# Eight images through four layers on one core: background work drawn evenly, and in chunk-sized tiles

## The chip, the cores and the metric

The kernel runs on one core of a Trainium2 chip. The metric is device time in microseconds (us), the median of three runs. The engines are PE (TensorE, matrix products, with weight loads shown as PEld), DVE (VectorE), ACT (ScalarE), POOL (GpSimd) and SP (SyncE); POOL and SP here mostly issue DMA transfers. All data are fp32.

## What is computed

The input is x of shape (8, 384, 32, 32): 8 images, 384 channels, 32 x 32 pixels. Four layers follow each other. Cut to what matters:

```python
# layer 0: Mamba in two directions, plus a gated 3x3 depthwise convolution
xn = rmsnorm(x, norm_w)
u, z = split(in_proj(xn))
u = silu(causal_conv1d(u, 4 taps))
dt, Bm, Cm = split(x_proj(u))
delta = softplus(dt_proj(dt) + dt_b)
# twice: over the pixels in order and in reverse
h[t] = exp(delta * A) * h[t-1] + (delta * u) * Bm     # 16 states a channel, scanned over 1024 pixels
y = (sum over states of h * Cm + u * D) * silu(z)
x1 = x + res_scale * (sigmoid(dwconv3x3(xn)) * xn + scale_mod * out_proj(y_forward + y_backward))
# layer 1, for each image: conv block, linear attention, MLP
x1 = conv1x1(bn(dwconv3x3(conv1x1(bn(x1))))) + x1
x2 = x1 + proj(linear_attention(qkv(x1)))
x2 = x2 + mlp(layernorm(x2))                          # 384 -> 1536 -> 384, GELU
# layer 2: seven depthwise kernels (13x13 and dilated ones), each with its batch norm, summed
# layer 3: 1x1 convolution + skip, 13x13 depthwise convolution + scaled skip, GELU
```

Layers 0 and 1 work image by image. Layers 2 and 3 work on all images at once, after the last image, as matrix products with Toeplitz matrices that are built from the convolution kernels.

## The kernel before

The scan of layer 0 is the backbone: 48 units an image (2 directions, 2 halves of 512 pixels, 3 chunks of 128 channels, 4 groups of states). A unit is, on DVE, a product, a scan and a second product, each over 2048 columns, with four ACT exponentials ahead and four small PE reductions behind:

```python
                da = das[i % len(das)]
                for j in range(4):
                    nc.scalar.activation(
                        da[:, SEG * j + 1 : SEG * (j + 1)], dlt[:, j, :], AF.Exp,
                        scale=neg_a[:, 4 * c + j, r : r + 1],
                    )
                du = sp.tile([P, 4 * SEG + 1], FP, tag="du", name=f"du_{b}_{i}", bufs=4)
                # ... first / last / carry cut
                nc.vector.tensor_mul(
                    flat(1)[:, :, 0:HALF], vt, bct[r][:, 0:1, :].to_broadcast([P, 4, HALF])
                )
                if pend is not None:
                    product(pend)
                if d == 0:
                    s = slice(0, 4 * SEG)
                    nc.vector.tensor_tensor_scan(du[:, s], da[:, s], du[:, s], 0.0, ALU.mult, ALU.add)
                else:
                    s = slice(1, 4 * SEG + 1)
                    nc.vector.tensor_tensor_scan(
                        du[:, s][:, ::-1], da[:, s][:, ::-1], du[:, s][:, ::-1], 0.0, ALU.mult, ALU.add
                    )
            # product(), called one unit later:
                nc.vector.tensor_mul(dv, dv, cct[:, 1:2, :].to_broadcast([P, 4, HALF]))
                for j in range(4):
                    nc.tensor.matmul(
                        acc[32 * j : 32 * j + 32, :], selt, dv[:, j, :],
                        start=False, stop=(r == NR - 1), skip_group_check=True,
                    )
```

Everything else of layers 0 and 1 is background: generators that issue a piece and yield its cost. `front(b)` is the input side of an image (norm, in_proj, convolutions, deltas), `layer1(b)` the second layer, `fold()` puts norms into weights and, at its end, makes the Toeplitz sources for layers 2 and 3 with `kernels()`. The loop over images draws them beside the scan:

```python
        for _ in front(0):
            tick()
        tick(everything=True)
        rounds = 4 * NC * NR
        for b in range(B):
            work = []
            if b + 1 < B:
                work.append((front(b + 1), 94))
            if b == 0:
                work.append((fold(), 30))
            if b > 0:
                work.append((layer1(b - 1), 290))
            need = sum(n for _, n in work)
            steps = (cost for g, _ in work for cost in g)
            done = 0
            for i, _ in enumerate(scan(b)):
                tick()
                while done < need * (i + 1) / rounds:
                    cost = next(steps, None)
                    if cost is None:
                        break
                    done += cost
            for _ in steps:
                tick()
            tick(everything=True)
        for _ in layer1(B - 1):
            tick()
        tick(everything=True)
```

The last part of `kernels()` copies windows of the merged kernels, DRAM to DRAM, 64 transfers of 24 x 32 x 224 elements, with a yield of cost 0:

```python
        NP = 24
        for g_d, t_d in ((g2_d, tp2_d), (g3_d, tp3_d)):
            for at in range(0, C // 2, NP):
                for q in range(2):
                    for e in range(2):
                        one_k = g_d[2 * at + e, q]
                        win = bass.AP(
                            one_k.tensor, one_k.offset,
                            [[4 * TG * (KP // 2), NP], [KP // 2, H], [1, TP]],
                        )
                        lo = 2 * H * q + H * e
                        nc.gpsimd.dma_start(t_d[at : at + NP, lo : lo + H, :], win)
                    yield 0
```

The background's tiles: half images with three chunks in one `a6` buffer, chunks in `t2`, weights in `w`.

```python
N_A6, N_T2, N_W, N_IM = 7, 10, 5, 6
# ...
        def t2(name):
            return sp.tile([P, HALF], FP, tag="t2", name=name, bufs=N_T2)

        def a6(name):
            return sp.tile([P, NC, HALF], FP, tag="a6", name=name, bufs=N_A6)

        def wtile(ap, name):
            t = sp.tile([P, NC, C], FP, tag="w", name=name, bufs=N_W)
            nc.gpsimd.dma_start(t, ap.rearrange("(k p) o -> p k o", p=P))
            return t
# ... in front(b):
            for e in range(2):
                w = wtile(inproj_t[:, e * C : (e + 1) * C], f"win_{b}_{e}")
                for h in range(2):
                    t = a6(f"uz_{b}_{e}_{h}")
                    for m in range(NC):
                        ps = psum(f"in_{b}_{e}_{m}_{h}")
                        dense(ps, w, m, xn[h])
                        if e == 0:
                            nc.scalar.copy(t[:, m, :], ps)
                        else:
                            nc.scalar.activation(t[:, m, :], ps, AF.Silu)
                        yield 3
                    if e == 0:
                        nc.gpsimd.dma_start(uo[:, :, 3 + h * HALF : 3 + (h + 1) * HALF], t)
                    else:
                        nc.gpsimd.dma_start(zv[b][:, :, bass.ts(h, HALF)], t)
# ... in layer1(b):
            for h in range(2):
                for m in range(NC):
                    ps = psum(f"c2_{b}_{m}_{h}")
                    dense(ps, w, m, dws[h])
                    t = t2(f"c2_{b}_{m}_{h}")
                    nc.scalar.activation(t, ps, AF.Identity, bias=biasc[:, m, :])

                    def residual(o=xx[h][:, m, :], t=t):
                        nc.vector.tensor_add(o, o, t)

                    defer(0, residual)
                    yield 3
# ... and at the end of each half's MLP:

                def last(h=h, acc=acc):
                    for m in range(NC):
                        o = xx[h][:, m, :]
                        nc.vector.scalar_tensor_tensor(
                            o, acc[m], vec("mlp_b2", m), o, ALU.add, ALU.add
                        )
                        # ... store to x2, cut
                defer(0, last)
```

Pieces that end on DVE are deferred (`defer(n, fn)`): they are issued n + 1 ticks later, and a tick comes with each scan unit. A scheduler then sets the final order on each engine, in which instructions wait for buffers and data in that engine's own queue.

## Time and profile before

| what | value |
|---|---|
| median of 3 runs | 6233.76 us (6221.53 to 6239.03) |
| span of the profiled execution | 6238.1 us |
| instructions in it | 52842 |
| DMA | 425913 packets, 1060.24 MB, mean 170 GB/s |
| mean granted TensorE clock | 0.864 of full speed |
| DVE scans (L771 and L774) | 2 x 192, 4.43 us each |
| DVE products (L764 and L686) | 2 x 384, 2.28 us each |
| first scan of images 0 to 7 at | 239, 721, 1475, 2087, 2699, 3310, 3922, 4531 us |

The page gives each engine's busy time as a share of the span, then 40 slices of it: a digit is the busy share of a slice in tenths. PEclk is the granted clock of TensorE, in tenths. An engine that is idle costs nothing unless the work that ends last waits for it. In views of stretches, a row is: from and to in us, its length, then busy time and number of instructions of PE, PEld, DVE, ACT and POOL, the granted clock, the busy share of the 16 DMA engines, and GB/s. In the view of waits, a row is: who waited, `<-` for whom, us in total, how many times, and the longest. The view of one line gives durations in ns (least, median, most), its waits, and, for a transfer, the time from issue to landing.

### The profile page before, as it was taken

Reading aid. Unit: us, or ns where it says so; the run is one execution under the profiler, and the core shown is the slowest. Engines: PE = TensorE matmul, PEld = TensorE weight load, DVE = VectorE, ACT = ScalarE, POOL = GpSimd, SP = SyncE. Lnnn points to the kernel's source line nnn. Section 1 sums busy time; section 2 is a strip of 40 time slices with the busy share of each in tenths; the row PEclk is TensorE's granted clock in tenths of the full one; section 3 lists DMA queues with packets and bytes.
Section 4 is the critical chain, followed back from the end, with each engine's and each line's share of the span. In section 5 each row is a group of like instructions: output and inputs, shape, how many; then the busy total and the mean of one; then the engine's idle time right before and its main releaser. Section 6 shows DMA issues by size and latency. Waiting matters only on the chain. (4 is left out here: it accounts for less than half of the span.)

```text
span 6238.1 us, 52842 instructions
## 1 busy us (share of the span) xinstructions
PE 4982.4 (80%) x19054; PEld 2193.0 (35%) x19054; DVE 4002.6 (64%) x2768; ACT 2789.8 (45%) x3891; POOL 1134.3 (18%) x1781
## 2 busy tenths in 40 slices
PE   4665407888789978898889789978989779898899
PEld 1111202333233323332333233323323224398498
DVE  0599943797779777977897789778978941000200
ACT  1655414455745574557355745574544523000211
POOL 4210223101210121013101310131010010111133
PEclk8776557899788978997899789979989889899999
DMA  9664696435643564466446643664363341399699
GB/s 294 203 193 135 213 306 195 146 122 152 228 144 122 158 224 142 139 161 228 126 146 174 217 134 124 186 219 127 122 181 109 131 118 41 79 221 216 208 215 198
DMA packets 425913, 1060.24 MB, mean 170 GB/s; under 512 B 58141, under 2 KB 108549, under 8 KB 425653
## 3 DMA queue, kind: packets, MB, share of 16 engines
q0 software_dynamic: 185792, 679.20, 37.6%
q1 hardware_dynamic: 210192, 354.31, 18.5%
q10 hardware_dynamic: 29668, 23.36, 1.6%
q8 instruction: 151, 2.47, 0.2%
q14 instruction: 110, 0.89, 0.0%
HBM read 807.16 MB, written 293.47 MB: 176 GB/s over the span
## 5 line engine op out<-in xcount | busy, mean ns | idle before, releaser
L751 ACT ACTIVATE da<-dlt,neg_a 128x512 f32<-128x512 f32 x1536 | 1000.2, 712 | 1063.4 <-DVE du L774 556.6
L764 DVE TENSOR_TENSOR du<-vr,bct 128x2048 f32<-128x2048 f32 x384 | 874.3, 2284 | 15.8 <-DMA vr<-v_d 9.8
L686 DVE TENSOR_TENSOR du<-du,bct 128x2048 f32<-128x2048 f32 x384 | 877.5, 2286 | 3.8
L771 DVE TENSOR_TENSOR_SCAN du<-da,du 128x2052 f32<-128x2052 f32 x192 | 849.1, 4427 | 40.5 <-ACT da L751 37.2
L774 DVE TENSOR_TENSOR_SCAN du<-da,du 128x2052 f32<-128x2052 f32 x192 | 848.2, 4426 | 6.2
L688 PE MATMUL acc<-du,selt 128*32 128x512 f32 x3072 | 606.8, 690 | 279.3 <-DVE du L686 279.3
L1000 PE MATMUL mo<-hm,w 128*128 128x512 f32 x1152 | 558.4, 626 | 61.8 <-ACT hm L998 59.1
L490 PE MATMUL mf<-ln,w 128*128 128x512 f32 x1152 | 551.3, 613 | 0.6 <-DVE ln L986 0.6
L499 PE MATMUL lc<-lc_i,t 96*32 96x512 f32 x1152 | 258.7, 860 | 170.4 <-DMA lc_i<-xn_d 167.6
L490 PE MATMUL in<-xn,win 128*128 128x512 f32 x576 | 264.4, 616 | 134.1 <-DMA win<-in_inproj_t 124.5
L499 PE MATMUL c<-ut,t 128*32 128x512 f32 x768 | 250.1, 804 | 141.1 <-ACT dl L650 54.8
L1000 PEld LDWEIGHTS mo<-hm,w 128*128 128x128 f32 x1152 | 219.2, 197 | 380.9 <-issue 246.3
L499 PE MATMUL dw<-dw_i,t3b 96*32 96x512 f32 x1152 | 265.9, 827 | 106.0 <-DMA dw_i<-h_d 95.4
L490 PEld LDWEIGHTS mf<-ln,w 128*128 128x128 f32 x1152 | 219.9, 196 | 321.5 <-issue 318.3
L312 PE MATMUL cv_b<-xt_b,toep 128*64 128x256 f32 x2688 | 302.4, 385 | 36.2 <-DMA xt_b<-xp_d 17.3
L688 PEld LDWEIGHTS acc<-du,selt 128*32 128x32 f32 x3072 | 100.1, 116 | 630.0 <-DVE du L686 359.4
L312 PE MATMUL cv_a<-xt_a,toep 128*64 128x256 f32 x2688 | 300.1, 383 | 24.6 <-issue 24.5
L312 PEld LDWEIGHTS cv_b<-xt_b,toep 128*64 128x64 f32 x2688 | 291.9, 194 | 47.2 <-issue 41.6
L998 ACT ACTIVATE hm<-mf,biasf 128x512 f32<-128x512 f32 x192 | 130.4, 687 | 397.9 <-PE mf L490 396.9
L312 PEld LDWEIGHTS cv_a<-xt_a,toep 128*64 128x64 f32 x2688 | 291.2, 194 | 33.1 <-issue 32.2
L751 ACT ACT_TABLE_LOAD x217 | 278.4, 1283 | 8.2 <-DVE du L771 4.5
L595 DVE TENSOR_TENSOR lg<-lg,xn 128x512 f32<-128x512 f32 x48 | 32.9, 686 | 338.9 <-ACT lg L592 338.9
(212 smaller groups left out, 6183.4 us busy)
## 6 DMA issues: line engine op xcount, KB each, us to landing
dlt<-dl_d SPq DMA_DIRECT2D x384, 256.0 KB, 5.8
vr<-v_d SPq DMA_DIRECT2D x384, 256.0 KB, 4.6
bct<-bc_d SPq DMA_DIRECT2D x256, 256.0 KB, 4.1
ut<-u_d POOLq DMA_DIRECT2D x192, 257.5 KB, 4.9
lc_i<-xn_d POOLq DMA_DIRECT2D x192, 228.8 KB, 5.8
dw_i<-h_d POOLq DMA_DIRECT2D x192, 228.8 KB, 4.3
tp_d<-g_d POOLq DMA_DIRECT2D x64, 672.0 KB, 20.1
w<-w_d POOLq DMA_DIRECT2D x64, 576.0 KB, 4.7
```

The costliest lines, as they stand in the source:

```text
L312: nc.tensor.matmul(ps[2 * H * e : 2 * H * (e + 1), 0:BW], tp[:, 2 * (g % (GB // 2)) + e, :, :, t].rearrange("p c j -> p (c j)"), rhs, star ...
L490: nc.tensor.matmul(ps, w[:, k, m * P : (m + 1) * P], rhs[k] if isinstance(rhs, list) else rhs[:, k, :], start=(k == 0), stop=(k == NC - 1),)
L499: nc.tensor.matmul(ps[32 * j : 32 * j + 32, :], lhs(j, i), rhs(j, i), start=(i == 0), stop=(i == taps - 1), skip_group_check=True,)
L595: nc.vector.tensor_mul(rows(lc), rows(lc), xn[h][c])
L686: nc.vector.tensor_mul(dv, dv, cct[:, 1:2, :].to_broadcast([P, 4, HALF]))
L688: nc.tensor.matmul(acc[32 * j : 32 * j + 32, :], selt, dv[:, j, :], start=False, stop=(r == NR - 1), skip_group_check=True,)
L751: nc.scalar.activation(da[:, SEG * j + 1 : SEG * (j + 1)], dlt[:, j, :], AF.Exp, scale=neg_a[:, 4 * c + j, r : r + 1],)
L764: nc.vector.tensor_mul(flat(1)[:, :, 0:HALF], vt, bct[r][:, 0:1, :].to_broadcast([P, 4, HALF]))
L771: nc.vector.tensor_tensor_scan(du[:, s], da[:, s], du[:, s], 0.0, ALU.mult, ALU.add)
L774: nc.vector.tensor_tensor_scan(du[:, s][:, ::-1], da[:, s][:, ::-1], du[:, s][:, ::-1], 0.0, ALU.mult, ALU.add)
L998: nc.scalar.activation(hm, ps, AF.Gelu, bias=biasf[:, NC * i + f, :])
L1000: nc.tensor.matmul(acc[m], wb[:, f, m * P : (m + 1) * P], hm, start=(i == 0 and f == 0), stop=(i == FF // C - 1 and f == NC - 1),)
```

## The change

The aim is to give each scan unit about the same background. The input side of the next image and the second layer of the previous one are now drawn side by side, whichever has used the smaller share of its cost, with costs set to 108 and 310 in place of 94 and 290, and drawn up by the last unit but one. The Toeplitz part leaves `fold()` for a generator of its own, `prepare()`, of cost 64, that runs beside image 1, with 2 a yield. So that both kinds of background can be alive at once, half-image tiles become chunks: `uz`, `xr` and `fr` take `t2` buffers, and each chunk has its own transfer. The scan's small tiles get a pool of their own (`s2`). To pay for this, there is one weight buffer less, one `bct` buffer less, and a narrower zero tile, so that pads are cleared in pieces of 384 columns. The residual of `c2` is issued a tick later, and forced before its first reader.

```diff
-N_A6, N_T2, N_W, N_IM = 7, 10, 5, 6
+N_A6, N_T2, N_S2, N_W, N_IM = 7, 11, 3, 4, 6
 ...
                         lo = 2 * H * q + H * e
                         nc.gpsimd.dma_start(t_d[at : at + NP, lo : lo + H, :], win)
-                    yield 0
+                    yield 2
 ...
-        zero = wp.tile([P, HALF], FP, tag="zero", name="zero")
+        zero = wp.tile([P, C + NC + 1], FP, tag="zero", name="zero")
         nc.gpsimd.memset(zero, 0.0)
         for i in range(2):
             for t, n in ((xn_d, IMG), (u_d, UL), (h_d, IMG)):
                 pads = t[i].rearrange("(c p) i -> p c i", p=P)
                 for c in range(NC):
-                    for a in range(0, n, HALF):
-                        e = min(n, a + HALF)
+                    for a in range(0, n, C):
+                        e = min(n, a + C)
 ...
+        def s2(name):
+            return sp.tile([P, HALF], FP, tag="s2", name=name, bufs=N_S2)
 ...
-                    t = a6(f"uz_{b}_{e}_{h}")
                     for m in range(NC):
                         ps = psum(f"in_{b}_{e}_{m}_{h}")
                         dense(ps, w, m, xn[h])
+                        t = t2(f"uz_{b}_{e}_{h}_{m}")
                         if e == 0:
-                            nc.scalar.copy(t[:, m, :], ps)
+                            nc.scalar.copy(t, ps)
+                            nc.gpsimd.dma_start(uo[:, m, 3 + h * HALF : 3 + (h + 1) * HALF], t)
                         else:
-                            nc.scalar.activation(t[:, m, :], ps, AF.Silu)
+                            nc.scalar.activation(t, ps, AF.Silu)
+                            nc.gpsimd.dma_start(zv[b][:, m, bass.ts(h, HALF)], t)
                         yield 3
-                    if e == 0:
-                        nc.gpsimd.dma_start(uo[:, :, 3 + h * HALF : 3 + (h + 1) * HALF], t)
-                    else:
-                        nc.gpsimd.dma_start(zv[b][:, :, bass.ts(h, HALF)], t)
 
 
             t3 = tapw(taps3, f"t3_{b}")
             for h in range(2):
-                xr = a6(f"xr_{b}_{h}")
-                nc.gpsimd.dma_start(xr, xv[b][:, :, bass.ts(h, HALF)])
                 for c in range(NC):
+                    xr = t2(f"xr_{b}_{h}_{c}")
+                    nc.gpsimd.dma_start(xr, xv[b][:, c, bass.ts(h, HALF)])
                     ps = conv3(xn_d, b % 2, h, c, t3, f"lc_{b}_{h}_{c}")
                     lc = t2(f"lg_{b}_{c}_{h}")
                     nc.scalar.activation(lc, ps, AF.Sigmoid, bias=vec("dw_b0", c))
 
                     def local(h=h, c=c, lc=lc, xr=xr):
                         nc.vector.tensor_mul(rows(lc), rows(lc), xn[h][c])
-                        nc.vector.scalar_tensor_tensor(
-                            xr[:, c, :], lc, rs, xr[:, c, :], ALU.mult, ALU.add
-                        )
-                        if c == NC - 1:
-                            nc.gpsimd.dma_start(x1v[b][:, :, bass.ts(h, HALF)], xr)
+                        nc.vector.scalar_tensor_tensor(xr, lc, rs, xr, ALU.mult, ALU.add)
+                        nc.gpsimd.dma_start(x1v[b][:, c, bass.ts(h, HALF)], xr)
 
 ...
-                fr = a6(f"fr_{b}_{h}")
-                nc.sync.dma_start(fr, x1v[b][:, :, cols])
                 w = wtile(outproj_t, f"wo_{b}_{h}")
                 for m in range(NC):
                     ps = psum(f"op_{b}_{m}_{h}")
                     dense(ps, w, m, g)
-                    nc.vector.scalar_tensor_tensor(
-                        fr[:, m, :], ps, rsm, fr[:, m, :], ALU.mult, ALU.add
-                    )
-                nc.gpsimd.dma_start(x1v[b][:, :, cols], fr)
+                    fr = t2(f"fr_{b}_{h}_{m}")
+                    nc.sync.dma_start(fr, x1v[b][:, m, cols])
+                    nc.vector.scalar_tensor_tensor(fr, ps, rsm, fr, ALU.mult, ALU.add)
+                    nc.gpsimd.dma_start(x1v[b][:, m, cols], fr)
 
 ...
-                        t = sp.tile([P, 2, HALF], FP, tag="bct", name=f"bct_{b}_{d}_{h}_{e}", bufs=5)
+                        t = sp.tile([P, 2, HALF], FP, tag="bct", name=f"bct_{b}_{d}_{h}_{e}", bufs=4)
 ...
+
+        def prepare():
             large = lambda name: sp.tile([P, NC * C], FP, tag="w", name=name, bufs=N_W)
             yield from kernels(t2, large)
 ...
-                    defer(0, residual)
+                    res[h].append(defer(1, residual))
 ...
+                for e in res[h]:
+                    force(e)
 ...
-                work.append((front(b + 1), 94))
+                work.append([front(b + 1), 108, 0])
+            if b > 0:
+                work.append([layer1(b - 1), 310, 0])
             if b == 0:
-                work.append((fold(), 30))
-            if b > 0:
-                work.append((layer1(b - 1), 290))
-            need = sum(n for _, n in work)
-            steps = (cost for g, _ in work for cost in g)
+                work.append([fold(), 30, 0])
+            if b == 1:
+                work.append([prepare(), 64, 0])
+            need = sum(n for _, n, _ in work)
             done = 0
             for i, _ in enumerate(scan(b)):
                 tick()
-                while done < need * (i + 1) / rounds:
-                    cost = next(steps, None)
+
+                while work and done < need * (i + 1) / (rounds - 1):
+                    w = min(work, key=lambda w: w[2] / w[1])
+                    cost = next(w[0], None)
                     if cost is None:
-                        break
+                        work.remove(w)
+                        continue
+                    w[2] += cost
                     done += cost
-            for _ in steps:
-                tick()
+            for w in work:
+                for _ in w[0]:
+                    tick()
```

More of the change, by code (lines that the diff above doesn't have):

```diff
@@ L478, in defer, with force @@
         def defer(n, fn):
-            late.append([n, fn])
+            e = [n, fn]
+            late.append(e)
+            return e
+        def force(e):
+            if e in late:
+                late.remove(e)
+                e[1]()
         def tick(everything=False):
@@ L695, in product @@
                 if d == 0:
-                    yt = t2(f"yt_{b}_{h}_{c}")
+                    yt = s2(f"yt_{b}_{h}_{c}")
                     nc.scalar.copy(yt, acc)
@@ L699, in product @@
                     return
-                zt = t2(f"zr_{b}_{h}_{c}")
+                zt = s2(f"zr_{b}_{h}_{c}")
                 nc.sync.dma_start(zt, zv[b][:, c, cols])
@@ L742, in scan @@
                     acc = accp.tile([P, HALF], FP, tag="acc", name=f"acc_{b}_{d}_{h}_{c}")
-                    yt = t2(f"y0_{b}_{d}_{h}_{c}")
+                    yt = s2(f"y0_{b}_{d}_{h}_{c}")
                     nc.sync.dma_start(yt, (udv if d == 0 else yfv)[b][:, c, cols])
@@ L858, in layer1 @@
             w = wtile(c2_d, f"c2_{b}")
+            res = [[], []]
             for h in range(2):
```

## The prediction

> **What bounds the kernel now.** I read the page first. Its line of busy times and its slices say that no engine is full:
>
> ```profile
> PE 4982.4 (80%) x19054; PEld 2193.0 (35%) x19054; DVE 4002.6 (64%) x2768; ACT 2789.8 (45%) x3891; POOL 1134.3 (18%) x1781
> ...
> PE   4665407888789978898889789978989779898899
> DVE  0599943797779777977897789778978941000200
> PEclk8776557899788978997899789979989889899999
> DMA  9664696435643564466446643664363341399699
> ```
>
> The fine structure repeats every four slices, and slice 6 (about 780 to 940 us) is a hole in PE and DVE while DMA is full. So the eight images are the unit to read in. I placed the cuts at the first forward scan (L771) of each image and asked for the busy time of each stretch:
>
> ```profile
> core 0: us, PE busy (x) PEld busy (x) DVE busy (x) ACT busy (x) POOL busy (x), PEclk, DMA share, GB/s
> 0.00:239.00 239.00, 109.84 (x326) 34.84 (x326) 30.62 (x83) 63.76 (x88) 92.56 (x161) 0.78 0.84 263
> 239.00:721.00 482.00, 276.48 (x928) 80.97 (x929) 470.31 (x312) 275.17 (x388) 76.14 (x134) 0.69 0.55 181
> 721.00:1475.00 754.00, 480.06 (x1570) 179.02 (x1569) 494.55 (x347) 312.49 (x441) 158.83 (x240) 0.77 0.62 193
> ...
> 2096.00:2708.00 612.00, 525.65 (x1658) 191.04 (x1658) 492.25 (x314) 343.71 (x467) 103.69 (x173) 0.88 0.53 164
> ...
> 4541.00:5055.00 514.00, 431.06 (x1363) 163.29 (x1362) 452.17 (x264) 245.04 (x340) 52.22 (x80) 0.91 0.44 132
> ```
>
> Image 0 has only the next image's input side beside its scan and is DVE-bound (470 of 482). Image 1 takes 754. Images 2 to 6 take 610 to 621 each, with PE at 526 and DVE at 492: 120 us of DVE idleness per image. Image 7 takes 514. Then 356 for the last second layer and 827 for the convolutions. Within one steady image, by quarters of its 48 scan units:
>
> ```profile
> 2096.00:2274.00 178.00, 152.43 (x502) 53.83 (x503) 127.20 (x87) 94.78 (x120) 40.62 (x67) 0.88 0.64 190
> 2274.00:2449.00 175.00, 138.87 (x439) 41.96 (x434) 126.37 (x83) 104.56 (x151) 41.66 (x78) 0.80 0.58 185
> 2449.00:2587.00 138.00, 125.72 (x429) 53.99 (x427) 125.19 (x89) 72.10 (x110) 7.19 (x11) 0.94 0.33 112
> 2587.00:2708.00 121.00, 108.62 (x299) 41.27 (x296) 113.49 (x58) 72.26 (x88) 14.22 (x19) 0.96 0.54 155
> ```
>
> The first half, where the leftover of the MLP and all of the input side run, is slow (178 and 175) at a lower granted clock; the second half is near DVE's own pace. What DVE waits for in that image:
>
> ```profile
> DVE xx L1009 <- PE mo L1000: 24.2, 1, 24.2
> DVE du L763 <- PE acc L688: 20.8, 5, 6.8
> DVE xx L867 <- ACT c L864: 16.8, 6, 5.3
> DVE dl L661 <- ACT sp L656: 16.8, 3, 13.1
> DVE lg L595 <- ACT lg L592: 11.9, 4, 7.4
> ```
>
> All but the second are a small background operation that stands in DVE's queue before its input is there, with the scan behind it. Last, the Toeplitz copies of image 1:
>
> ```profile
> L239 POOL DMA_DIRECT2D tp_d<-g_d x64: 828/835/886, 722.2 to 919.5; - x64
> ...
> DMA to landing us min/median/max: 5.2/20.1/28.8
> ```
>
> Between 755 and 945 us DMA is busy 0.96 of the time and DVE 89 of 190 us; the longest single waits there are 130 us (DVE for the sigmoid) and 126 us (PE for `win`).
>
> **What the Trainium skill says.** "Trace Analysis", section Optimization Strategy: where the most-contended engine changes over time, "performance may be improved by interleaving those regimes". The trace agrees that there are such regimes: the quarters above. "TensorE: Matmul & The Clock Gate", Part 1, has the clock depend on recent PE activity; the trace agrees in direction (0.80 in the quarter with PE at 79%, 0.96 in the one at 90%). "DMA: Bandwidth & Descriptors", Issuing engines are not separate DMA queues: all queues share 16 engines, so spreading the copies frees no bandwidth, it only moves it; here 64 copies of 672 KB, 43 MB. "ScalarE: Activation LUTs", What ACT_TABLE_LOAD costs: about 1283 ns a switch; the trace has 1283.
>
> **The change part by part.**
>
> *Even draw.* The built instruction orders (no times in them) show what the scheduler made of it. Before, the input side's PE work of image b+1 stands in units 3 to 15 and layer 1 from unit 15 into unit 3 of the next image. After, in images 3 to 6, the input side runs from unit 1 to unit 47, the MLP from 26 to 47, and its last matmuls end at unit 0 of the next image. The work is the same. PE work at full clock in a steady image, busy times clock by quarter: 152.4 x 0.88 + 138.9 x 0.80 + 125.7 x 0.94 + 108.6 x 0.96 = 468 us. Quarters 3 and 4 get through 118.2/138 = 104.3/121 = 0.86 of it per us with DVE at 91 to 94%. If the whole image ran like that: 468/0.86 = 544 us, in which DVE's 492 would be 90%. The evenness is not perfect: one lump of about 56 us of PE work stands between the reductions of units 8 and 9 in the order. DVE can run only some three units ahead (four `du` buffers), about 35 us, so it loses some 20 us there, of which I count 11. Steady image: 555 against 613, four of them (3 to 6): gain 4 x 58 = 232.
>
> *Image 7.* It has only layer 1 beside it. It loses the leftover MLP of the image before at its start (a wait of 24 us as above): 514 to 490, gain 24.
>
> *Toeplitz in image 1, and what it drags along.* Gained is the hole: 754 - 613 = 141 at most. But the new order is not even there. The copies stand in clumps of 6 to 8 at units 23, 27, 31, 35 and 47, and the last ten or so lie in image 2. Around them PE's order has lumps: I tallied the matmuls between successive reductions with the mean times of the steady image (0.92 us a built 512-column matmul, 0.44 an `lc` one, 0.7 a `kv` one) and got about 62, 64, 66 and 64 us in image 1 and 54, 94 and 90 us in image 2, to which some 90 us of PE work of image 1 is pushed. Each costs DVE its length less 35: 27 + 29 + 31 + 29 + 19 + 59 + 55 = 249. With DVE's own 2 x 492, and 65 for DMA crowding (the 43 MB at the 297 GB/s of the hole are 145 us of DMA on top of 0.53 x 613 = 325 in a 640 us image, 0.73 share; I take under half as felt): 984 + 249 + 65 = about 1300 for the two, against 754 + 621 = 1375. Gain 75.
>
> *Chunk tiles.* Same bytes, more transfers: 165 to 185 issues on the POOL queue per steady image, 20 x 0.6 us = 12 us of POOL, which is busy 104 of 612. Hidden. The half-image tiles no longer hold `a6` buffers while background of both kinds is alive, which is what makes the even draw possible. One fewer weight buffer (4) and one fewer `bct` buffer cost no wait that I can find in the order.
>
> *Table loads.* 81 to 91 per steady image in the order, 10 x 1.28 = 13 us of ACT at 56% busy: hidden.
>
> *Residual deferred by one tick.* Takes part of the 16.8 us of `xx L867`; already in the rate above.
>
> *Before image 0.* The smaller zero tile makes 12 more pad transfers, and chunks 14 more issues: 27 x 0.6 = 16 us of POOL in a 239 us stretch that waits mostly for landings; I add 6. Image 0 stays at DVE's pace, 482. The last layer and convolutions stay at 1183.
>
> Sum: 245 + 482 + 1300 + 4 x 555 + 490 + 1183 = 5920, on a span that was 6238; the median was 5 us lower than the span, which I leave.
>
> **The rivals.**
>
> *PE becomes the bound and nothing is won in the steady images.* PE is busy 526 of 612 now. At an unchanged clock it would need 526 us and some friction: 590 an image, total about 6060. For it: PE at 90% or more in the best windows already. Against: the low clock and waits of the second quarter, which mixing should lift.
>
> *The clumps turn into a new hole.* If POOL, which issues its queue in order and waited 110 us in total for earlier Toeplitz copies, holds up image loads behind each clump, images 1 and 2 together cost 1450 instead of 1300: total 6070.
>
> *Everything mixes well.* Steady images at 520 (DVE 95%), images 1 and 2 at 1180: 245 + 482 + 1180 + 2080 + 475 + 1183 = 5645. For it: image 0 shows DVE at 98% beside background. Against: image 0 has less than half the PE work.
>
> *More `t2` users starve the pool.* 11 buffers serve the chunks, the MLP's activations and the deltas at once; a wait for a buffer would show as ACT waiting for POOL or DMA. It would cost tens of us per image and bring the total to 6150.
>
> **Range and chances.** The steady images decide: four images at plus or minus 20 us are 80, images 1 and 2 plus or minus 100, the rest 20; together about 130 either way, slightly wider on the slow side since two rivals lie there: 5780 to 6080. Faster by over 2% means under 6109. Only the starved pool, or two of the slow rivals together, lead above it: 0.89 faster, 0.09 within 2%, 0.02 slower.
>
> **What would show it.** In the changed profile: no window near 780 to 940 us with DMA full and PE empty; starts of images 3 to 7 about 555 apart, with their quarters within 20 us of each other; the wait `DVE xx <- PE mo` of 24 us per image gone; mean granted clock above 0.90 in images 3 to 6; images 1 and 2 still the longest, about 650 each, with PE lumps in them. I am wrong if the steady images stay over 590, if image 1 is under 580, or if the last 1183 us change by more than 15.

## The result and the profile after

| | before | after |
|---|---|---|
| median of 4 runs each | 6236.40 us (6221.53 to 6279.01) | 6067.57 us (6063.13 to 6068.56) |
| ratio | | 0.9717, 95% interval 0.9669 to 0.9765 |
| mean granted clock | 0.864 | 0.877 |

The change gains 169 us where 316 were predicted. The time lies inside the range (5780 to 6080), near its slow end. From first scan to first scan of consecutive images, and then to the end, in us:

| | start | 0 | 1 | 2 | 3 | 4 | 5 | 6 | 7 | last layer and convolutions |
|---|---|---|---|---|---|---|---|---|---|---|
| before | 239 | 483 | 753 | 621 | 612 | 611 | 612 | 610 | 514 | 1183 |
| predicted | 245 | 482 | 1300 for 1 and 2 | | 555 | 555 | 555 | 555 | 490 | 1183 |
| after | 247 | 479 | 738 | 711 | 559 | 553 | 551 | 557 | 486 | 1187 |

Every entry is within 5 us of the prediction but one: images 1 and 2, 1449 us for 1300. (The list of first scans ahead of the prediction is 9 to 10 us early from image 3 on; they stand at 2096, 2708, 3319, 3931 and 4541 us, and the row "before" is worked out from these.) The slices of the page, of 152 us each, show both halves of this:

```profile
PE   3665546675479989898998999898978879798899
...
DVE  0499995565674897998899789978989921000200
...
PEclk8676767787789989898999899898989979899999
```

Counted from 1, slices 15 to 32 are images 3 to 7, with PE and DVE at seven tenths or more throughout. Slices 7 to 13 are where DVE's 9s are missing, in images 1 and 2. The hole of before (DMA full, PE and DVE empty) is not among them: from 780 to 940 us DVE is full now, and DMA at 0.60.

Stretches of the changed kernel from first scan to first scan, for images 1, 2 and 4 (columns as in the prediction):

```profile
726.00:1464.00 738.00, 451.38 (x1451) 162.48 (x1452) 486.90 (x342) 286.79 (x400) 145.49 (x224) 0.76 0.54 172
1464.00:2175.00 711.00, 567.67 (x1835) 209.61 (x1835) 502.11 (x329) 388.93 (x521) 137.79 (x232) 0.88 0.55 168
2733.00:3287.00 554.00, 494.24 (x1664) 179.90 (x1663) 492.65 (x316) 358.41 (x480) 113.54 (x194) 0.94 0.60 182
```

Image 4 (2733 to 3287) takes 554 us with DVE at its old 493 and PE at 494 instead of 526, at a clock of 0.94 instead of 0.88: 526 x 0.88 and 494 x 0.94 are both about 463 us at full clock, so it is the same work at a higher clock. The Trainium skill ("TensorE: Matmul & The Clock Gate", Part 1) has the clock follow the recent activity of PE. The trace agrees in direction: 0.94 with PE busy for 89% of the image, 0.88 with 86% before. Its largest DVE wait, in the view of waits (who, for whom, us in total, times, longest):

```profile
DVE du L764 <- PE acc L693: 21.4, 4, 15.4
```

The 24.2 us for `mo` of the MLP are gone (0.4 us are left). The wait of 21 us for the reduction is the lump between units 8 and 9, here 15.4 us once.

Images 1 and 2 are no less busy on DVE (487 and 502), but idle for 251 and 209 us. Cut into eighths, the pair reads as follows (the first, the second and the seventh):

```profile
726.00:910.00 184.00, 90.52 (x302) 24.07 (x302) 183.93 (x143) 66.38 (x102) 35.32 (x59) 0.67 0.59 191
910.00:1095.00 185.00, 115.35 (x420) 55.86 (x421) 81.39 (x47) 59.36 (x91) 27.34 (x40) 0.79 0.43 140
...
1820.00:1998.00 178.00, 174.67 (x684) 75.42 (x682) 88.67 (x77) 103.79 (x134) 38.96 (x69) 0.97 0.42 131
```

For the first 184 us DVE is full and PE gets work for half of the time, at a clock of 0.67: too little background stands in the order there. In the next eighth DVE is busy for 81 of 185 us. In the seventh PE is at 98% and DVE at 50%. What DVE waits for in image 1, and the largest single wait of image 2, as DVE's timeline has it (start, duration, operation, and in brackets the idle time before it with its releaser):

```profile
DVE du L766 <- PE acc L693: 91.5, 4, 33.6
DVE kv L912 <- PE kvs L906: 35.8, 1, 35.8
DVE du L764 <- PE acc L693: 30.9, 2, 17.4
```
```profile
1871.89 0.06 DVE L766 MEMSET du<- 128x4 f32 x1 [52.64 <-PE acc L693]
```

In PE's timeline from 1819 to 1872 us there are `kv`, `kvs` and `in` matmuls back to back, and the next reduction (`acc`) comes after them. It is the first of the two large lumps that the built order holds in image 2 (94 and 90 us in the prediction), and the wait is 52.6 us where the prediction had 94 - 35 = 59. POOL, on the other hand, hardly waits for its copies:

```profile
L239 POOL DMA_DIRECT2D tp_d<-g_d x64: 831/862/1017, 759.9 to 1597.0; - x64
...
  DMA tp_d<-g_d: 5.1, 3
...
DMA to landing us min/median/max: 5.4/9.4/20.9
```

The 64 copies are issued over 837 us now, and land in 9.4 us (before 20.1); 5.1 us of waiting in all. So the second rival had the right number for images 1 and 2 (1450), and the wait on which it rested, POOL's for its own copies, is not there. That loads near the copies land late all the same is shown further down.

### The profile page after: what moved, and what is told of

It reads as the page before. It is cut to its first block, busy times and chain, and to the rows that moved or that the text cites. A ratio compares the mean times of both kernels' runs of the same rounds, so it can differ in the third digit from the quotient of the medians.

```text
span 6066.8 us, 53234 instructions
## 1 busy us (share of the span) xinstructions
PE 4850.3 (80%) x19054; PEld 2142.6 (35%) x19054; DVE 3998.1 (66%) x2768; ACT 2852.0 (47%) x3941; POOL 1216.0 (20%) x1953
## 5 line engine op out<-in xcount | busy, mean ns | idle before, releaser
L693 PE MATMUL acc<-du,selt 128*32 128x512 f32 x3072 | 570.9, 687 | 324.2 <-DVE du L691 308.4
L509 PE MATMUL dw<-dw_i,t3b 96*32 96x512 f32 x1152 | 252.3, 784 | 99.0 <-DMA dw_i<-h_d 87.8
L312 PE MATMUL cv_a<-xt_a,toep 128*64 128x256 f32 x2688 | 302.9, 386 | 30.1 <-issue 24.2
L500 PE MATMUL in<-xn,win 128*128 128x512 f32 x576 | 284.2, 628 | 28.8 <-ACT uz L588 22.6
L754 ACT ACT_TABLE_LOAD x195 | 250.2, 1283 | 67.3 <-DVE du L777 41.1
L509 PE MATMUL lc<-lc_i,t 96*32 96x512 f32 x1152 | 188.4, 671 | 65.0 <-DMA lc_i<-xn_d 64.2
L327 DVE COPY yt<-cv_a 128x256 f32<-128x256 f32 x48 | 20.4, 425 | 309.6 <-PE cv_a L312 309.6
L500 PE MATMUL h<-xx,c 128*128 128x512 f32 x288 | 143.6, 659 | 81.3 <-DMA xx<-x_d 81.3
```

Of the source, the lines that this page charges most:

```text
L312: nc.tensor.matmul(ps[2 * H * e : 2 * H * (e + 1), 0:BW], tp[:, 2 * (g % (GB // 2)) + e, :, :, t].rearrange("p c j -> p (c j)"), rhs, star ...
L327: nc.vector.tensor_copy(hold["t"][:, g % GB, :], ps)
L500: nc.tensor.matmul(ps, w[:, k, m * P : (m + 1) * P], rhs[k] if isinstance(rhs, list) else rhs[:, k, :], start=(k == 0), stop=(k == NC - 1),)
L509: nc.tensor.matmul(ps[32 * j : 32 * j + 32, :], lhs(j, i), rhs(j, i), start=(i == 0), stop=(i == taps - 1), skip_group_check=True,)
L693: nc.tensor.matmul(acc[32 * j : 32 * j + 32, :], selt, dv[:, j, :], start=False, stop=(r == NR - 1), skip_group_check=True,)
L754: nc.scalar.activation(da[:, SEG * j + 1 : SEG * (j + 1)], dlt[:, j, :], AF.Exp, scale=neg_a[:, 4 * c + j, r : r + 1],)
```

## The experiments

All are variants of one of the two kernels. The durations of an image come from each kernel's trace, as in the table above; the ratio is to the kernel before, run beside it. That kernel's median was 6228 to 6241 us in the three groups of runs, so a difference between totals of different runs is good to some 13 us. "Lumps" are tallied in the built order as in the prediction: PE work between successive reductions, and of each what exceeds 35 us, summed over an image. A steady image after the change has 20 us of it, so the tally bears on an image's time by how far it exceeds 20. In the texts quoted below, which stood before each run, letters stand for theories where they are used: Q for POOL's queue with the copies in it, O for the order of the instructions in which the copies stand, B for the bytes that the copies move.

### Where the loss is made: the copies' queue, their spread, the costs, the draw

**Copies on ACT's queue**, nothing else (the scheduler then builds another order):

```diff
-                        nc.gpsimd.dma_start(t_d[at : at + NP, lo : lo + H, :], win)
+                        nc.scalar.dma_start(t_d[at : at + NP, lo : lo + H, :], win)
```

> The changed kernel with one word changed: the 64 Toeplitz copies are issued on ACT's queue instead of POOL's. Same bytes, same place in the program, same cost of 2 a yield. In the built order the lumps of PE work in images 1 and 2 (up to 65 and 90 us between successive reductions) are gone: no more than 35 us in image 1, and image 2 stands like images 3 to 6. Theory O (the order the scheduler made around the copies costs the time): images 1 and 2 take about 2 x 570 in place of 738 + 711, total about 5760. Theory B (the copies' 43 MB and the full DMA engines cost it at run time): images 1 and 2 still take 1400 or more, total about 6050. A third possibility: ACT, in whose queue the copies now stand, issues its exponentials late; then image 1 is long with DVE waiting for the exponentials (da), and image 2 is short.

Measured 5887.17 us, 0.944 (0.9409 to 0.9472): images 1 and 2 take 715 and 550. Image 2 is steady, so its 157 us of excess belong to the copies' place and not to the bytes or the tiles. Image 1's order has no lump over 35 us at all, and it still takes 161 us more than a steady one. The view of waits for DVE in it shows another cause:

```profile
DVE du L774 <- ACT da L754: 58.5, 4, 43.7
...
DVE du L767 <- DMA vr<-v_d: 25.5, 4, 19.6
DVE du L767 <- DMA bct<-bc_d: 19.4, 7, 5.3
```

`da`, the scan's coefficient, is late on ACT (58.5 us), as the third possibility of the text above has it, but the copies in ACT's queue are the smaller part of that. A copy takes 0.75 us of the queue at best and 6.8 us at most, and ACT waits behind copies for 16.3 us before its exponentials, 10.7 us of it once. The single wait of 43.7 us (783 to 827 us) starts at a transfer: `da` stands in ACT's order behind the copying of `dw`, which waits for PE, and PE waits 19.7 us for the load of `dw_i`. That load waits 12.5 us for the store of its source `h_d`, which was issued at 785.3 us beside two copies and took 13.2 us to land. The rest of DVE's waits are loads of the scan and small waits for PE; what made those late was not separated.

**All copies at once again**, in the new kernel (no cost per copy, all of them drawn at the first step):

```diff
-                    yield 2
+                    yield 0
-                work.append([prepare(), 64, 0])
+                work.append([prepare(), 1, 0])
```

> The changed kernel with all 64 Toeplitz copies drawn at once at the start of image 1, as before the change (yield 0), and everything else as changed. In the built order image 1 has lumps of 96, 90 and 41 us at units 23, 27 and 31, image 2 none beyond the steady ones. Theory O: the hole of some 150 to 190 us comes back in image 1, but image 2 falls to about 555; images 1 and 2 together about 1310, total about 5930, so spreading the copies over the POOL queue has cost time. Theory B: spreading is worth what it hides, so this kernel is slower than the changed one, 6100 or more.

Measured 5874.22 us, 0.9414 (0.937 to 0.9458). Stretches of images 1 and 2, and what PE waited for longest in image 1:

```profile
729.00:1447.00 718.00, 490.56 (x1626) 176.28 (x1619) 496.98 (x354) 337.78 (x458) 168.08 (x262) 0.80 0.66 204
1447.00:2001.00 554.00, 494.91 (x1659) 179.03 (x1658) 492.25 (x316) 357.73 (x480) 113.50 (x194) 0.94 0.59 180
```
```profile
PE h L500 <- DMA xx<-x_d: 90.0, 2, 83.3
```

The hole of the kernel before is back for PE in image 1: from 763 to 957 us, with the copies, PE is busy for 36 of 194 us (it waits 83 us once for a load of `xx`), at a DMA share of 0.94. DVE is busy for 156 of them and pays at the end of the hole and after it, with two waits for the reduction of 67.7 and 55.9 us. Image 1 costs 719 us. But image 2 costs 554. So spreading the copies, the part of the change that was to close the hole, costs 193 us (6067.57 - 5874.22): image 1 with the copies spread is no better than with the hole (738), and image 2 is lost as well (711). Without it the change would have gained 362 us.

**The kernel before with the new costs alone:**

```diff
-                work.append((front(b + 1), 94))
+                work.append((front(b + 1), 108))
-                work.append((layer1(b - 1), 290))
+                work.append((layer1(b - 1), 310))
-                while done < need * (i + 1) / rounds:
+                while done < need * (i + 1) / (rounds - 1):
```

> The kernel before, with the three numbers of the draw alone put right: 108, 310 and rounds - 1 (still one generator after the other, half-image tiles, copies in one go). If the even draw is what shortens the steady images: 612 falls only by the 24 us wait for the MLP's leftover, to about 588, total about 6234 - 6 x 24 = 6090. If the wrong costs alone were the trouble: steady images near 555 as in the changed kernel, total about 5900. The hole in image 1 stays in both.

Measured 6259.17 us, 1.0027 (1.0014 to 1.0041). The steady images take 611 to 619, where the two forecasts were 588 and 555. Finishing earlier does remove the wait for the leftover of the MLP, and other waits grow by as much: 37.4 us for the reduction and 36.2 us for the softplus in one image, where the kernel before had 20.8 and 16.8. Nothing of the gain is here.

**The new kernel with the old draw**, first the input side, then the second layer:

```diff
-                    w = min(work, key=lambda w: w[2] / w[1])
+                    w = work[0]
```

> The changed kernel with the generators drawn one after the other (input side, then layer 1, then the copies) in place of side by side; chunks, pools and costs as changed. In the built order steady images have one lump of 73 us where the changed kernel has one of 55 and, in sum, 38 us over 35 against 20. If drawing side by side brings the steady gain: images 3 to 6 about 585 in place of 554, total about 6070 with the copies at the end of image 1 and a lump of 148 us in image 2. If the chunk tiles and the right costs bring it: steady images within 8 of 554.

Measured 6166.49 us, 0.9882 (0.9842 to 0.9923). Image 4 of this kernel:

```profile
2683.00:3284.00 601.00, 521.35 (x1659) 186.91 (x1658) 493.93 (x315) 354.28 (x474) 112.94 (x193) 0.90 0.55 168
```

Steady images take 600 us (585 was forecast if the draw makes the gain), the tiles, pools and costs of the change notwithstanding. Of the 58 us that a steady image gains (612 to 554), drawing side by side makes 46, all the rest 12. The Trainium skill ("Perfetto Trace Analysis", Optimization Strategy), which the prediction quoted, has mixing regimes as something that may help; here it is worth 46 of 600 us. Images 1 and 2 go the other way: they take 638 and 715 us in this order, 96 us less together than with the even draw.

### What about the copies costs it: order, queue, bytes

**Copies late, on SP.** The merges that need SBUF stay in image 1; the copies are handed to the scheduler after everything else that competes with them, two for every second step of the last second layer, and it fits them in where there is room:

```diff
-                        nc.gpsimd.dma_start(t_d[at : at + NP, lo : lo + H, :], win)
+                        nc.sync.dma_start(t_d[at : at + NP, lo : lo + H, :], win)
+        toep = prepare()
-                work.append([prepare(), 64, 0])
+                work.append([islice(toep, 7), 1, 0])
-        for _ in layer1(B - 1):
+        for n, _ in enumerate(layer1(B - 1)):
             tick()
+            if n % 2 == 0:
+                next(toep, None)
+        for _ in toep:
+            pass
```

> The changed kernel with the Toeplitz copies written last in the program (beside the last second layer) and issued on SP's queue. The scheduler then fits them into its free places: 28 in image 1, 31 in image 2, 5 in image 3, one to a scan unit, and PE's order has no lump over 46 us in image 1. Theory O: the cost of the copies is the order alone, so image 1 takes about 580 and image 2 about 555; total about 5740. Theory B: in all three arrangements so far image 1 took 715 to 738, some 165 over a steady image, because the copies' DMA time (some 145 us) has to be paid somewhere; then images 1 and 2 together take about 1110 + 150, total about 5880.

Measured 5723.03 us, 0.9196 (0.9176 to 0.9215): the fastest of all, faster than both kernels. In the built order the copies do not end up late. 28 stand in image 1, 31 in image 2 and 5 in image 3, about one to a scan unit; in the trace they are issued 29, 28 and 7 to an image. Its images 1 and 2, DVE's two largest waits in image 1, and the copies (issue duration least, median, most in ns; first and last start):

```profile
720.00:1280.00 560.00, 497.30 (x1659) 180.21 (x1660) 505.45 (x364) 358.79 (x479) 119.43 (x204) 0.91 0.68 219
1280.00:1832.00 552.00, 480.31 (x1626) 175.22 (x1625) 484.21 (x306) 348.46 (x468) 108.67 (x188) 0.93 0.69 215
```
```profile
DVE xx L874 <- ACT c L871: 15.7, 4, 10.3
DVE du L765 <- PE acc L694: 13.2, 4, 8.5
```
```profile
L240 SPq DMA_DIRECT2D tp_d<-g_d x64: 749/786/4744, 752.6 to 1961.0; - x64
```

57 of the 64 copies are issued in these two images, at a DMA share of 0.68 and 0.69, and the images take 560 and 552 us, together 4 us more than two steady ones (2 x 554). Image 3, with the other seven, takes 553. So the bytes cost next to nothing when they come evenly. Spreading frees no bandwidth, as the prediction has it, but in this run bandwidth was not short. The tally of lumps is 11 and 22 us, as in a steady image.

**The same, on POOL**; the edit is to the kernel with late copies:

```diff
-                        nc.sync.dma_start(t_d[at : at + NP, lo : lo + H, :], win)
+                        nc.gpsimd.dma_start(t_d[at : at + NP, lo : lo + H, :], win)
```

> As the kernel with the copies written last, but on POOL's queue: the scheduler spreads them over images 1, 2 and half of 3, with lumps that sum to 37, 75 and 59 us over 35 (20 in a steady image). Theory O: images 1 to 3 take about 575, 610 and 595, total about 5830, slower than on SP by the lumps. Theory B: no difference to the copies on SP, since the bytes are the same and POOL waits little for copies.

Measured 5896.56 us, 0.9477 (0.9446 to 0.9507), images 1 to 3 at 606, 632 and 591. Against 554 that is 52, 78 and 37 too long; the tallies exceed 20 by 17, 55 and 39. It lies between the two theories, and most of the excess (111 of 167 us) is what the tally of the order gives.

**Copies on SP, left in their place:**

```diff
-                        nc.gpsimd.dma_start(t_d[at : at + NP, lo : lo + H, :], win)
+                        nc.sync.dma_start(t_d[at : at + NP, lo : lo + H, :], win)
```

> The changed kernel with the Toeplitz copies issued on SP's queue, at the changed kernel's place in the program (2 a yield beside image 1). All 64 copies stay in image 1, and the built order keeps lumps of PE work there: 119, 51, 72 and 60 us between successive reductions, 162 us over 35 in sum; image 2 has none (4). Theory O (order): image 1 takes about 560 + 150 = 710, image 2 about 550, total about 5870, although the queue is the one on which the late copies cost nothing. Theory Q (the copies sit in POOL's ring ahead of the background's loads, and SP does not have that): image 1 about 580, total about 5740.

Measured 5952.07 us, 0.9562 (0.9528 to 0.9595): images 1 and 2 take 805 and 532. Image 1, DVE's largest waits in it, and the copies' issues:

```profile
724.00:1528.00 804.00, 529.60 (x1676) 188.56 (x1676) 503.32 (x369) 331.66 (x458) 124.72 (x211) 0.78 0.60 188
```
```profile
DVE dl L666 <- ACT sp L661: 59.3, 6, 22.6
DVE kv L912 <- PE kvs L906: 57.4, 1, 57.4
DVE xx L873 <- ACT c L870: 45.3, 6, 33.3
```
```profile
L239 SPq DMA_DIRECT2D tp_d<-g_d x64: 761/2497/10497, 756.4 to 1465.7; - x64
```

This pair shows that the place decides. With the same queue and the same 64 copies, images 1 and 2 take 560 and 552 us in one order and 805 and 532 in the other, and the busy share of DMA in image 1 is lower here (0.60 for 0.68). Image 1 holds all 64 copies here and 29 there, so what differs is how densely they stand, and with them the rest of the order. Theory Q falls: the loss needs no copies in POOL's queue. Theory O's number was too low as well, 805 for 710. In this order the lumps of image 1 come to 162 us (119, 51, 72 and 60 long), and an issue takes 2.5 us in the median and up to 10.5, since the copies stand in clumps. DVE's waits for the reduction and for `kvs` are only 88 us (16.2 + 14.9 + 57.4). The loads of `dlt`, which SP also issues, come late (ACT waits 49 us for them), and so do `sp` and `c` of ACT (DVE waits 59 and 45 us).

**The copies a whole image earlier** (beside image 0, where PE is idle for 200 us):

```diff
-            if b == 1:
+            if b == 0:
                 work.append([prepare(), 64, 0])
```

> The changed kernel with the copies (and the merging of the kernels) drawn beside image 0 in place of image 1, still on POOL. In the built order 12 of the 64 copies are left in image 1, but PE's order in image 1 has the lumps that image 2 of the changed kernel has (90, 90, 32, 32). Theory O: image 0, where PE has much to spare, takes about 500, and image 1 about 690 although nearly all copies are done before it; total about 5910. Theory B: image 0 takes about 480 + 150, and image 1 about 580; total about 5930. The two totals are alike, the images are not.

Measured 5974.38 us, 0.9602 (0.9569 to 0.9635): images 0 to 2 take 629, 663 and 556. Image 1 has 12 of the copies in the built order and a tally of 111 us, 91 over the steady one, and is 109 too long. Image 0 has no lumps (tally 6) and is 150 too long: there theory O's number fell. Where eight copies clump, at units 27, 35 and 47 of the order, the loads behind them are late (PE waits 62.6 us for the input of the local convolution, DVE 38.9 us for `lg` that follows from it). Another 38.7 us of DVE's waits there are for products of `fold()`, which runs beside the same image. So lumps of PE work are not the only harm of a clump: the loads behind it seem to be another.

### Does the even draw need the chunk tiles?

**The kernel before with the new draw and the spread copies only**; tiles, pools, weight buffers and residual as before (`prepare()` as in the new kernel, `yield 2`):

```diff
-                work.append((front(b + 1), 94))
+                work.append([front(b + 1), 108, 0])
 ...
+                    w = min(work, key=lambda w: w[2] / w[1])
+                    cost = next(w[0], None)
```

> The kernel before with the new draw alone: both generators side by side, costs 108 and 310, the copies in a generator of their own beside image 1 with 2 a yield; the half-image tiles, pools and buffer counts are those of before. In the built order its steady images have 16 us over 35 in lumps (20 in the changed kernel, 28 before), and image 2 has 31 where the changed kernel has 130. If the chunk tiles are what makes the even draw possible: steady images stay near 610. If the draw alone does it: steady images about 552, images 1 and 2 about 690 and 560, total about 5900, faster than the changed kernel.

Measured 6030.32 us, 0.9697 (0.9672 to 0.9722). Its images 3 to 6 take 550 to 570 us with half-image tiles, against 551 to 559 with chunks. Images 1 and 2 take 786 and 634, far from the 690 and 560 expected: image 2 is some 74 us longer than this kernel's steady ones, with a tally of only 31.

**The kernel before with only the late copies on SP:**

```diff
-                        nc.gpsimd.dma_start(t_d[at : at + NP, lo : lo + H, :], win)
+                        nc.sync.dma_start(t_d[at : at + NP, lo : lo + H, :], win)
 ...
+        toep = kernels(t2, lambda name: sp.tile([P, NC * C], FP, tag="w", name=name, bufs=N_W))
-            yield from kernels(t2, large)
+            yield from islice(toep, 7)
 ...
-        for _ in layer1(B - 1):
+        for n, _ in enumerate(layer1(B - 1)):
             tick()
+            if n % 2 == 0:
+                next(toep, None)
+        for _ in toep:
+            pass
```

> The kernel before with the Toeplitz copies alone changed: written last and issued on SP, so that the scheduler fits them in one by one over images 1 and 2; draw, tiles and buffers as before. Its lumps in image 1 sum to 33 over 35 (before: 65 and the hole), elsewhere as before. The hole of 142 us goes and nothing else: images 1 to 6 about 612 each, total about 6090.

Measured 6079.2 us, 0.9766 (0.9735 to 0.9797): image 1 takes 591 for 753, images 2 to 6 are as before (604 to 619).

**Both edits in the kernel before**, new draw and late copies on SP:

> The kernel before with the new draw and with the copies written last on SP, but half-image tiles and all buffer counts as before. Against the 5723 of the changed kernel with the same copies it shows what the chunk tiles bring. If they bring nothing, as the kernel with the new draw alone suggests (steady images 550 to 570): images 1 to 6 about 557, total within 20 of 5723. If chunks shorten the steady image: 5740 to 5780.

Measured 5740.26 us, 0.9224 (0.9194 to 0.9255), images 1 to 6 at 555 to 571. Its interval overlaps that of the late copies in the new kernel (0.9176 to 0.9215): what the chunks, pools and residual bring together cannot be told from nothing in the total. By image there is a hint of more: in the two traces images 1 to 6 are 48 us shorter in sum with chunks (3330 for 3378 us), and what comes before and after them is 26 us longer. That is one execution of each kernel.

The gains add up. On the new kernel's side: even draw 362 us (the run with copies at once, which has the old hole), late copies in the old kernel 157 (6236.40 - 6079.2), sum 519; both together 513 (6236.40 - 5723.03), the same within the 13 us above.

## Why the prediction was right and where it was wrong

**The total.** It lies in the range because all other stretches came out within 5 us. The miss of images 1 and 2, 149 us, is above the 100 that the prediction gave them either way, and it is as good as the whole miss of the total (148).

**Steady images, image 7, the ends: right.** Predicted 555, measured 551 to 559; 490 against 486; 245, 482 and 1183 against 247, 479 and 1187. The working, same PE work at the pace of the better quarters with DVE at about 90%, is what the profile shows: DVE 493 of 554 is 89%. The sequential-draw run shows the draw as its cause. The clock of 0.92 to 0.94 in images 3 to 6 met "above 0.90", and the MLP wait went. More POOL issues and table loads were hidden, as said; POOL is at 114 of 554 and ACT at 358. On the cost of a table load the prediction gave half of what the Trainium skill ("ScalarE: Activation LUTs", What ACT_TABLE_LOAD costs) states: the page adds a drain of about 1380 ns to each switch. Here the drain does not show: at 76 of the 91 loads in image 4 the next instruction of ACT starts at most 1.4 us after the end of the one before the load, so the 1283 ns stand. (The 12 and 14 extra issues before image 0 are 26 and not 27, which changes nothing.) Only the evenness was overstated: the quarters of image 4 take 129, 155, 139 and 131 us, 26 apart and not within 20. The second has the most PE work (145 us of its 155).

**Images 1 and 2: the failed step.** It is the sum "984 + 249 + 65 = about 1300", which came out at 1449. Three terms, each against a run:

| term | predicted | measured | from |
|---|---|---|---|
| two images without lumps | 984 (DVE's own) | 1108 | 2 x 554, the steady image after |
| DMA crowding by 43 MB | 65 | 4 | late copies on SP, 57 of the 64 here: 560 + 552 less 1108 |
| lumps and clumps | 249 | 337 | what is left: 738 + 711 less 560 + 552 |

The first was a slip of reasoning: a steady image with the same even draw takes 555 by the prediction's own account, so DVE's 492 was not the base to add lumps to. The second was fear of a resource that has room when the copies come evenly.

The third had the mechanism right and mis-sized it: each lump was to cost "its length less 35", counting PE's own work alone. For the lump of 94 that is near what came out (52.6 us for 59). Over all, the waits that carry the name of the reduction or of `kvs` fall short: in image 1 they are 158 us, 135 above the steady image's 23 and near the 116 that its four lumps were given; in image 2 they are 85, 62 above, less than half of the 133 for its three. The loss is in the lumps all the same. Take the stretches from one reduction to the next around the seven lumps: 917 to 1005, 1011 to 1113, 1178 to 1264 and 1352 to 1460 us in image 1; 1573 to 1697, 1781 to 1871 and 1876 to 1955 us in image 2. DVE is idle in them for 381 of its 460 us of idleness in both images. In a steady image (image 4, 2827 to 2888 us) it is 24 of 61. So 333 of the 337 us lie there (381 less twice 24).

Two things hid them from the tally. First, the stretches last 677 us and PE is busy for only 478 of them, near the 494 that the seven lumps were given. For the other 199 us PE itself waits, most of it for ACT (`dw`, `uz`, `lg`, `hm`) and the rest for loads, of weights above all. Some loads are late there: between 1560 and 1700 us, where the last four copies are issued, `dlt` lands after 12.1 us (median) and a `w` after 16.0, against 6.4 and 4.5 in image 4. Second, in a lump DVE may also wait for the background that the lump produces. In the lump of 90 (1876 to 1955 us) PE is busy for 77 of 79 us and DVE for 43, but no wait for the reduction is over 7.0 us: DVE waits in small pieces for `qp`, `xx`, `ln` and `lg`, whose input comes from PE, directly or through ACT.

That image 2 is late because PE work of image 1 was pushed into it was not tested alone, but it fits the built order (601 us of PE work in place of 511 between its reductions); the variants of the new kernel with the even draw whose image 2 has a tally like a steady one (4 to 22 us) have it at 532 to 556.

**"Gained is the hole: 754 - 613 = 141 at most": a fair ceiling, and the wrong sign for the part.** The prediction saw that the copies' clumps would cost, but still gave images 1 and 2 "Gain 75"; they took 75 more than before (1449 for 1374). By the runs the spreading as built costs 193, and a spread that leaves the order even, as with the late copies, gives 151 (5874.22 - 5723.03).

**"Which is what makes the even draw possible": wrong.** The half-image tiles carry the even draw as well, at 550 to 570 us a steady image. The prediction took the purpose of the chunks from the diff and did not ask whether the scheduler needs them.

**The rivals.** Images 1 and 2 at 1450 came true, by instructions in the wrong place, not by POOL waiting for its copies (5.1 us). PE as the bound did not occur: at the higher clock PE needs 494 of 554 us, as much as DVE; 590 was this rival's number, and the sequential draw gives 600. A starved pool shows nowhere: the largest waits of ACT in image 4 are for the scan and for PE.

**What stays open.** Image 1 with the copies on ACT is 161 us too long without any PE lump. `da` on ACT is 58.5 us of DVE's waits, and the largest of them goes back to a transfer beside two copies. Whether the rest is the loads behind clumped copies too, as image 0 in the earlier-copies run suggests, was argued and not shown. Copies with fewer columns, which would separate the bytes in a clump from its issues, were not tried. How much of the 199 us that PE waits inside the lumps is due to late loads, and how much to ACT's own order, is not known either.

## What to carry to other kernels

With a static order per engine, a large background transfer harms by where it stands, not by its bytes: 43 MB cost 3 us over three images in one order (560 + 552 + 553 less 3 x 554), and some 160 to 340 us in others. So tally, between the instructions that the bound engine needs next, the work that every other engine has in its order, and look for clumps of transfers in it too, since loads behind them may pay. A tally of one engine's own work does not say how long it will take: here the seven lumps held 478 us of PE work and lasted 677 us. And when a change has two aims, here an even draw and a closed hole, run each alone: one gave 362 us and the other took 193.

## What was unexpected of the hardware

The issue of one copy of 672 KB is not a fixed cost: 0.75 us on ACT or SP alone, but up to 6.8 us on ACT and 10.5 us on SP (2.5 in the median) where several stand together; on POOL 0.86 us and never over 1.02. On SP in the changed kernel's place, 45 of the 53 copies that follow another within 10 us take over 1.1 us, and none of the other 11. Work of the same engine behind such an issue waits: ACT stood still for 10.7 us once before an exponential, and for 16.3 us in all. And 0.68 to 0.69 of DMA busy over two images, 0.15 more than in a steady image of the kernel before, left DVE at 89% of its time, the same as at 0.60.
